# Block products of a row-tile pair formed with seven products instead of eight, in a fused autocorrelation and feed-forward kernel

## The chip, the cores and the metric

The kernel runs on one core of a Trainium2 chip, in float32 throughout. The metric is device time in microseconds, the median of several runs. Engines are named as the profile names them: PE (TensorE, the matmuls), DVE (VectorE), ACT (ScalarE), POOL (GpSimd) and SP (SyncE, which here only issues DMAs). They run beside each other, each in the order of its own instructions, and wait for each other on semaphores.

## The reference, cut to what matters

```python
def reference(x, w1q, a1, b1, w3q, a3, b3, w2q, a2, b2):      # x: (2, 2048, 1024)
    xn = _layernorm(x, axis=-1)
    # autocorrelation of each row, six best lags, weighted sum of the row shifted by them
    f = rfft(xn)
    corr = irfft(f * conj(f), n=1024)
    weights, delay = top_k(corr, 6)
    w = softmax(weights)
    s = sum_k(w[k] * xn[(t + delay[k]) % 1024])
    # gated feed-forward, weights repeated four times along the inputs, rank-2 additions
    q = lambda x, wq, A, B: x @ tile(wq, (1, 4)).T + 0.5 * (x @ A.T @ B.T)
    g = silu(q(silu(q(xn, w1q, a1, b1)) * q(xn, w3q, a3, b3), w2q, a2, b2))
    return x + s * g
```

The hidden width is 2752, a quarter of it 688, the row length 1024. There are 4096 rows.

## The kernel before

**Tiling.** Rows are taken 512 at a time, in 8 *macros* of 4 row tiles of 128. A macro's feed-forward works on columns: hidden values lie on partitions, the 512 rows along the free dimension. Because the weights repeat, the four quarters of the hidden vector are added up before the down product, so that it has an inner length of 688: five *chunks* of 128 (`zf[0]` to `zf[4]`) and a remainder of 48 with the two rank-2 rows, which is written twice, at partitions 0 and 64 (`zf[5]`).

**Steps.** A macro has 15 steps, written out in the last loop of the kernel. Steps 0 to 9 are `Ffn.up`: one chunk `c` in two steps, two quarters `j` in each step, four matmuls (0.86 us each) to a quarter. A quarter's two accumulators start from a *seed*, a scaled copy that ACT writes into the bank (L522); after the matmuls ACT takes Silu of the first (L549), DVE multiplies by the second (L551, "the z product"), and POOL adds the result into `zf[c]` (L554, L556). Step 10 is `up_rest`, the remainder in four accumulators (L573, L580, L590, L591). Steps 11 to 14 are `down(r)`, one row tile each: for both 512-column halves five matmuls of K=128 (L620) and one of K=64 (L631), then `out`: Silu on ACT (L642), times `s` on DVE (L643), plus `x` on POOL (L644), and the store. In the first of these steps `lora_mid` adds the rank-2 rows into `zf[5]` (L604, L607).

**Work between.** Each step has four lists of further work, `pre`, `mid`, `half` and `end`: ahead of the step's matmuls, after half of them, behind that, and behind the step. `plan` fills them by hand. They hold the next macro's norm (`stats`, `norm` with the folds `fold_a` and `fold_b`, `save` to DRAM twice over), its transposes (`turn`), the spectra (`power`: two matmul pairs, three ACT instructions, a DVE product and a POOL sum; every second one also joins two spectra, L386), and for each row tile `lags` (four matmuls, then the correlation row `corr`, L425 to L432, of which ACT writes the mirrored half) and `search` (MAX8 and FIND_INDEX8 on DVE). A row tile's six lags feed six gathers from DRAM (POOL's queue, L474, at most four in flight) and six weighted sums (`Gathers.sum`: the first on ACT, L488, five on DVE, L491); the list `sums` says how many are made at the half and at the end of each step. Macro 0 also makes its own spectra and searches (steps 0 to 5), and `lessen_part(c)` takes a row out of the first layer's weights, chunk by chunk (L137 on DVE, L138 on POOL).

**Buffers.** PSUM: two banks `ps` for transposes, spectra and lags, five `psf` (`full()`) for up and down accumulators, one `psu`. SBUF tiles with one tag share that tag's buffers. The order is the program's on each engine; DMAs of x, stores and weights are issued by SP, also in order, and a load waits there until its buffer is free.

Of the kernel before, what the change touches and what calls it, by code (L numbers as in the profile page):

```python
# [35 lines left out]
F32 = mybir.dt.float32  # L36
U32 = mybir.dt.uint32
I32 = mybir.dt.int32
AF = mybir.ActivationFunctionType
# [6 lines left out]
TOP = 6  # L46
# [22 lines left out]
def block_kernel(ctx: ExitStack, tc: tile.TileContext, x, w13t, w0t, w5t, w2t, a13, b13, b5, a2t, tf, ti, pick, out):  # L69
# [12 lines left out]
    p5 = pool("p5", ROLLS)  # L82
    small = pool("small", 3)
# [23 lines left out]
    w2_sb = const.tile([P, NC, L], F32)  # L107
    b5_sb = const.tile([P, 4], F32)
# [7 lines left out]
    b = const.tile([P, 513], F32, name="b")  # L116

    def constants():
        nc.gpsimd.memset(mhalf, -0.5)

        nc.scalar.activation(basef, mhalf, AF.Silu)
        nc.gpsimd.memset(euler, math.e)
        nc.gpsimd.memset(minus, -1.0)
        nc.gpsimd.memset(minus[0:1, :], 0.0)
        nc.gpsimd.memset(b[:, 512:513], 0.0)
        make_identity(nc, ident)
        nc.gpsimd.iota(base, pattern=[[0, 1]], base=0, channel_multiplier=2 * L)

    def fold_b(b, bcs):

        at = lambda first, par, n: bass.AP(b.tensor, b.offset + first, [list(b.ap[0]), [par, 2], [n, P]])
        nc.gpsimd.tensor_tensor(bcs[:, 0:2, :], at(0, 1, 2), at(512, -1, -2), ALU.subtract)
        nc.gpsimd.tensor_tensor(bcs[:, 2:4, :], at(2, -1, 2), at(510, 1, -2), ALU.add)
# [12 lines left out]
    def fold_lora(nat):  # L146

        pairs = p1.tile([P, 2, 8, 4], F32, tag="e2", name="a_pairs")
        nc.gpsimd.tensor_tensor(pairs, nat[:, 0], nat[:, 1], ALU.add)
        nc.gpsimd.memset(a13_sb, 0.0)  # L150
        whole = p1.tile([P, 8, 4], F32, tag="o2", name="a_whole")
        nc.gpsimd.tensor_tensor(whole[:, :2], pairs[:, 0, :2], pairs[:, 1, :2], ALU.add)
        nc.gpsimd.tensor_tensor(whole[:, 2:], pairs[:, 0, 2:], pairs[:, 1, 2:], ALU.subtract)
        nc.scalar.activation(a13_sb[:, :, :4], whole, AF.Copy, scale=0.125)


    class Corr:
# [25 lines left out]
        def norm(self, r, tags=("yc", "bcs")):  # L183
# [6 lines left out]
            yc = p1.tile([P, 4, P], F32, tag=tags[0], name=f"yc_{n}")  # L190
            bcs = p1.tile([P, 4, P], F32, tag=tags[1], name=f"bcs_{n}")
            nc.vector.tensor_tensor(a, xt[:, :512], xt[:, 512:], ALU.add)
            fold_a(a, yc, rest)
            nc.gpsimd.tensor_tensor(b[:, :512], xt[:, :512], xt[:, 512:], ALU.subtract)
# [43 lines left out]
        def lora_spread(self):  # L238
# [6 lines left out]
            self.u = p1.tile([P, NR], F32, tag="u", name=f"u_{self.m}")  # L245
# [79 lines left out]
        def lora_first(self, ffn):  # L325
# [3 lines left out]
            self.u = p1.tile([P, NR], F32, tag="u", name=f"u_{m}")  # L329
# [10 lines left out]
            for g, tags in enumerate((("ec", "e2"), ("zf2", "zf3"))):  # L340
                e = full(f"fe_{m}_{g}")
                self.wave(e, g, 0)
                ec, e2 = [p1.tile([P, NR], F32, tag=tag, name=f"{tag}_{m}_{g}") for tag in tags]
# [10 lines left out]
            nc.vector.tensor_copy(self.u, acc)  # L354
# [19 lines left out]
        def squares(self, g, ec, e2, o):  # L374
# [5 lines left out]
            o2 = p1.tile([P, NR], F32, tag="o2", name=f"o2_{m}_{g}")  # L380
# [3 lines left out]
            if g % 2:  # L384
                both = self.pwy if g == 1 else self.bT[:, 0:2, :]
                nc.gpsimd.tensor_tensor(both, both, to, ALU.add)  # L386

        def power(self, g):
# [4 lines left out]
            ec = p1.tile([P, NR], F32, tag="ec", name=f"ec_{m}_{g}")  # L393
            e2 = p1.tile([P, NR], F32, tag="e2", name=f"e2_{m}_{g}")
# [10 lines left out]
        def lags(self, r):  # L405
# [13 lines left out]
            corr = p1.tile([P, L], F32, tag="corr", name=f"corr_{n}")  # L419
# [43 lines left out]
    class Gathers:  # L463
# [15 lines left out]

        def sum(self, count):  # L480
            for _ in range(count):
                if not self.flying:
                    self.begin()
                st, r, k, g = self.flying.pop(0)
                w = st.w[:, r, k : k + 1]
                if k == 0:
                    s = self.s[st.m, r] = p3.tile([P, L], F32, tag="s", name=f"s_{st.m}_{r}")
# [6 lines left out]
    class Ffn:  # L494
# [69 lines left out]
        def up_rest(self, mid, half):  # L564
# [32 lines left out]
            nc.vector.tensor_tensor(last[:64, :], last[:64, :], zs[3][:64, :], ALU.add)  # L597

        def lora_mid(self):

            self.flush()
            last = self.zf[FULL]
# [6 lines left out]
        def down(self, r, mid, half):  # L609
            row = (self.m * RT + r) * P  # L610
            xs = []
            for d in range(2):
                xt = p2.tile([P, 512], F32, tag="x2", name=f"x2_{self.m}_{r}_{d}")
                nc.sync.dma_start(xt, x[row : row + P, d * 512 : (d + 1) * 512])
                xs.append(xt)
            accs = [full(f"y_{self.m}_{r}_{d}") for d in range(2)]
            rc = slice(r * P, (r + 1) * P)
            for d, acc in enumerate(accs):
                for c in range(FULL):
                    nc.tensor.matmul(  # L620
                        acc, lhsT=self.zf[c][:, rc], rhs=w2_sb[:, c, d * 512 : (d + 1) * 512], start=(c == 0), stop=False
                    )
                if d == 0:
                    if r == 0:
                        self.lora_mid()
                    mid()
                    half()

            for d, acc in enumerate(accs):
                at = slice(64 * d, 64 * d + 64)  # L630
                nc.tensor.matmul(  # L631
                    acc, lhsT=self.zf[FULL][at, rc], rhs=w2_sb[at, FULL, d * 512 : (d + 1) * 512], start=False, stop=True
                )
            return accs, xs

        def out(self, r, accs, xs, s):
            row = (self.m * RT + r) * P
            last = self.m == macros - 1 and r == RT - 1
            for d in range(2):
                cols = slice(d * 512, (d + 1) * 512)  # L640
                g = p2.tile([P, 512], F32, tag="g", name=f"g_{self.m}_{r}_{d}")
                nc.scalar.activation(g, accs[d], AF.Silu)  # L642
                nc.vector.tensor_tensor(g, s[:, cols], g, ALU.mult)  # L643
                (nc.vector if last else nc.gpsimd).tensor_tensor(g, g, xs[d], ALU.add)  # L644
                nc.sync.dma_start(out[row : row + P, cols], g)


    def plan(m, st, nxt, after, gathers, ffn_next):
# [3 lines left out]
        sums = [(1, 0)] * 7 + [(1, 2)] * 3 + [(1, 1), (0, 0), (2, 1), (2, 1), (0, 0)]  # L652
        sums[10] = (0, 0)
        sums[0], sums[1] = (0, 0), (1, 1)
        sums[8], sums[9], sums[11], sums[14] = (2, 1), (2, 1), (1, 0), (1, 0)
        if first:
            sums = [(0, 0)] * 7 + [(1, 1), (2, 1), (1, 1), (2, 2), (2, 2), (2, 1), (2, 1), (3, 0)]
            mid[0].append(st.odd_first)
            pre[1].append(lambda: st.power(2))
            mid[1].append(lambda: st.power(3))  # L660
            for r in range(RT):
                look(st, r, mid[2 + r], end[2 + r], gathers)
            mid[2 + RT].append(st.weights)
            for c in range(2, FULL + 1):
                pre[(0, 0, 1, 3)[c - 2]].append(lambda c=c: load_first(c))
                end[2 * c - 3].append(lambda c=c: lessen_part(c))
        else:
            end[0].append(st.weights)
        if nxt is not None:
            if first:  # L670
                loads, norms, turns = (None, None, None, 3), (0, 1, 4, 6), (mid[6], pre[7], mid[7], pre[8])
                stats = (half[0], half[1], end[2], half[5])

                tags = (("yc", "bcs"), ("zf4", "zf5"), ("e2", "o2"), ("yc", "bcs"))
            else:
                loads, norms, turns = (None, None, 1, 3), (0, 2, 4, 6), (pre[2], pre[4], pre[6], pre[8])
                stats = (half[0], end[1], end[3], end[5])
                tags = (("yc", "bcs"),) * RT
            for r in range(RT):
# [3 lines left out]
                end[norms[r]].append(lambda r=r: (nxt.norm(r, tags[r]), nxt.save(r)))  # L683
# [6 lines left out]
            pre[11].extend([nxt.again, nxt.lora_spread])  # L690
            for r in range(RT):
                look(nxt, r, mid[MID + 1 + r], end[MID + 1 + r], gathers)
# [243 lines left out]
```

## Time and profile before

| | |
|---|---|
| time, median of 3 runs | 1163.31 us (1163.22 to 1164.65) |
| the profiled execution's own time | 1167.36 us |
| its span, first to last instruction | 1165.6 us |
| granted PE clock, mean over the span | 0.994 of full speed |
| HBM read and written | 150.65 MB and 50.39 MB, 172 GB/s over the span |
| POOL's adds of L556 and L554 | 127.8 us and 51.8 us |
| POOL's folds L194, L132, L133 | 35.8, 25.5 and 28.8 us, 28 of each |
| POOL's joins L386 | 24.8 and 19.8 us, 8 of each |
| DVE's weighted sums L491 | 249.0 us, 160 of 1556 ns |

The page gives one profiled execution: busy time of each engine, the chain of work that ended last, the costliest groups of instructions by line and shape. A group's mean can hide two kinds of the same instruction, for instance alone and beside another engine, so single instructions are read from the timeline. PE is busy when a matmul is in flight; whether its clock was full is seen in the granted clock of a stretch. A float32 matmul of 128 x 512 shows as two records.

### The profile page before, as it was taken

To read this page: it belongs to the slowest core of one execution; us is meant where nothing else is said; L and a number is where in the kernel's file an instruction comes from. 1 tells how busy PE (TensorE), PEld (TensorE's weight loads), DVE (VectorE), ACT (ScalarE), POOL (GpSimd) and SP (SyncE) were. 2 spreads that over 40 slices of the span, in tenths; PEclk is the share of its full clock that TensorE was granted. 3 is DMA by queue.
4 is the path that set the end of the run, shared out by engine and by line. 5 is a ranking of instruction groups with operands and counts; after the bars stand their busy time and mean duration, and the time that the engine had idled before them with its cause. 6 is when DMAs were issued, how large, how long until landed. Compare 5 with 4: busy or idle time off the path is not lost.

```text
span 1165.6 us, 11210 instructions
## 1 busy us (share of the span) xinstructions
PE 1138.2 (98%) x3540; PEld 485.7 (42%) x3540; DVE 755.3 (65%) x1009; ACT 603.7 (52%) x1045; POOL 814.4 (70%) x675
## 2 busy tenths in 40 slices
PE   5999999999999999999999999999999999999997
PEld 4344344343444434444344433444344443444432
DVE  5587488665586746865577656785658765573455
ACT  4656623666346662566535664266633666344531
POOL 4778767877577884777767776787866877564653
PEclk9999999899999999999999999999999999999999
DMA  9941368534565435654355443754357534452334
GB/s 364 372 151 75 109 203 293 184 132 145 163 214 183 142 130 180 217 181 162 128 175 201 169 160 109 236 207 147 118 157 237 181 127 155 144 190 90 119 116 162
DMA packets 64915, 201.78 MB, mean 173 GB/s; under 512 B 7612, under 2 KB 7868, under 8 KB 64088
## 3 DMA queue, kind: packets, MB, share of 16 engines
q0 software_dynamic: 27648, 100.68, 26.9%
q1 hardware_dynamic: 37208, 100.39, 23.9%
q8 instruction: 28, 0.46, 0.2%
q14 instruction: 31, 0.25, 0.1%
HBM read 150.65 MB, written 50.39 MB: 172 GB/s over the span
## 4 chain that ended last, share of the span: by engine, by line
PE 87%; DVE 7%; POOL 2%; ACT 2%; issue 2%; DMA 0%; DVEq 0%; ACTq 0%; POOLq 0%
PE gu L544 44%; PE y L620 21%; PE u L527 4%; PE y L631 3%; PE gu L580 2%; PE t L216 2%; PE gu L573 2%; DVE s L491 1%; PE fe L369 1%; PE fe L372 1%; PE fo L369 1%; PE o L414 1%; PE fo L372 1%; PE ua L232 1%; PE e L414 1%
## 5 line engine op out<-in xcount | busy, mean ns | idle before, releaser
L544 PE MATMUL gu<-yT,w_sb 128*128 128x512 f32 x960 | 460.5, 601 | 0.1
L620 PE MATMUL y<-w_sb,zf 128*128 128x512 f32 x640 | 287.5, 597 | 0.5 <-ACT g L642 0.5
L544 PEld LDWEIGHTS gu<-yT,w_sb 128*128 128x128 f32 x960 | 176.8, 191 | 233.9 <-issue 214.4
L474 POOL DMA_INDIRECT roll<-scr,lag x192 | 230.2, 1199 | 47.4 <-issue 33.3
L491 DVE SCALAR_TENSOR_TENSOR s<-roll,w,s 128x1024 f32<-128x1024 f32 x160 | 249.0, 1556 | 7.2 <-DMA roll<-scr,lag 4.3
L551 DVE TENSOR_TENSOR z<-z,gu 128x512 f32<-128x512 f32 x160 | 109.2, 683 | 175.9 <-PE gu L544 118.0
L522 ACT ACTIVATE gu<-second,b_sb 128x512 f32<-128x512 f32 x320 | 207.6, 684 | 10.2 <-DVE z L551 9.3
L549 ACT ACTIVATE z<-gu 128x512 f32<-128x512 f32 x160 | 95.3, 596 | 177.8 <-PE gu L544 176.2
L620 PEld LDWEIGHTS y<-w_sb,zf 128*128 128x128 f32 x640 | 117.3, 190 | 147.8 <-issue 144.7
L644 POOL TENSOR_TENSOR g<-g,x 128x512 f32<-128x512 f32 x62 | 101.8, 1661 | 94.2 <-DVE g L643 88.5
L544 PE MATMUL gu<-yU,w_sb 128*128 128x512 f32 x320 | 163.8, 593 | 0.0
L556 POOL TENSOR_TENSOR zf<-zf,z 128x512 f32<-128x512 f32 x80 | 127.8, 1598 | 21.5 <-DVE z L551 20.3
L554 POOL TENSOR_TENSOR zf<-z,z 128x512 f32<-128x512 f32 x40 | 51.8, 1295 | 85.9 <-DVE z L551 84.2
L544 PEld LDWEIGHTS gu<-yU,w_sb 128*128 128x128 f32 x320 | 61.1, 191 | 77.2 <-issue 73.6
L643 DVE TENSOR_TENSOR g<-s,g 128x512 f32<-128x512 f32 x64 | 41.6, 690 | 67.5 <-ACT g L642 67.4
L450 POOL TENSOR_TENSOR e<-euler,e 128x6 f32<-128x6 f32 x32 | 45.8, 1431 | 41.8 <-DVE e L449 40.0
L642 ACT ACTIVATE g<-y 128x512 f32<-128x512 f32 x64 | 34.8, 593 | 77.3 <-PE y L631 59.6
L432 ACT COPY corr<-corr 128x511 f32<-128x511 f32 x32 | 19.8, 619 | 79.7 <-DVE corr L431 79.7
L527 PE MATMUL u<-z,a_sb 128*2 128x512 f32 (+1 forms) x384 | 52.9, 591 | 2.0 <-DVE z L551 2.0
L143 DVE SCALAR_TENSOR_TENSOR yc<-a,rest 128x256 f32<-128x256 f32 x28 | 41.6, 1487 | 5.3 <-POOL rest L188 2.0
L515 ACT ACTIVATE gu<-second,b_sb 64x512 f32<-64x512 f32 x64 | 43.9, 686 | 1.7
L418 ACT COPY oc<-o 128x258 f32<-128x258 f32 x32 | 12.0, 375 | 63.0 <-PE o L414 62.8
(167 smaller groups left out, 1358.9 us busy)
## 6 DMA issues: line engine op xcount, KB each, us to landing
scr<-x SPq DMA_DIRECT2D x64, 512.0 KB
x<-in_x SPq DMA_DIRECT2D x32, 512.0 KB
x<-in_x SPq DMA_DIRECT2D x64, 256.0 KB
out<-g SPq DMA_DIRECT2D x64, 256.0 KB
w_sb<-in_w13t SPq DMA_DIRECT2D x5, 1024.0 KB
second<-rows SPq DMA_DIRECT2D x14, 256.0 KB
w_sb<-in_w2t SPq DMA_DIRECT2D x1, 3072.0 KB
roll<-scr,lag POOLq DMA_INDIRECT x192, 5.7
```

What stands on the lines that cost most here:

```text
L450: nc.gpsimd.tensor_tensor(e, bass.AP(euler.tensor, euler.offset, [list(euler.ap[0]), [0, TOP]]), e, ALU.pow)
L474: nc.gpsimd.indirect_dma_start(out=g, out_offset=None, in_=st.scratch[r].rearrange("p (n o) -> (p n) o", o=1), in_offset=bass.IndirectOffs ...
L491: nc.vector.scalar_tensor_tensor(s, g, w, s, ALU.mult, ALU.add)
L522: nc.scalar.activation(acc, self.st.second[:, wi, :], AF.Copy, scale=b13_sb[:, c, q : q + 1])
L527: nc.tensor.matmul(self.u2[32 * j : 32 * j + 2, :], lhsT=a2_sb[:rows, 4 * c + j, :], rhs=z[:rows, :], start=(c == 0), stop=(c == FULL),)
L544: nc.tensor.matmul(acc, lhsT=w13_sb[:, c, 2 * j + wi, k, :], rhs=y, start=False, stop=(k == 1), skip_group_check=True,)
L549: nc.scalar.activation(z, accs[0], AF.Silu)
L551: nc.vector.tensor_tensor(z, z, accs[1], ALU.mult)
L554: nc.gpsimd.tensor_tensor(self.sum_of(c), zs[0], zs[1], ALU.add)
L556: nc.gpsimd.tensor_tensor(self.zf[c], self.zf[c], z, ALU.add)
L620: nc.tensor.matmul(acc, lhsT=self.zf[c][:, rc], rhs=w2_sb[:, c, d * 512 : (d + 1) * 512], start=(c == 0), stop=False)
L644: (nc.vector if last else nc.gpsimd).tensor_tensor(g, g, xs[d], ALU.add)
```

## The change

1. `down` and `out` of one row tile become `down_head`, `down_tail` and `out` of a *pair* of row tiles, q = 0 in steps 11 and 12, q = 1 in steps 13 and 14. Chunks 0 to 3 are treated as two 2 x 2 block products (chunks 0 and 1, chunks 2 and 3; blocks are two row tiles by two chunks and two chunks by two column halves), in the form of Winograd: seven products instead of eight, added in four banks. The copy of P1 to a second bank and of P7 to SBUF is ACT's, two sums into banks are DVE's. Chunk 4 and the remainder stay as they are; the two remainder matmuls of a pair now take two row tiles instead of two halves.
2. The combinations of the left side (`mix`: four DVE instructions of 128 x 256 for each pair of chunks) are made at the ends of steps 8 and 9; those of the weights once, on POOL (`mix_weights`: four instructions of 128 x 1024), in macro 0's steps 6 and 7.
3. `b` and `fold_b` move from POOL to DVE; `join` is split from `squares` and moves from POOL to DVE, to step 10 (step 1 in macro 0).
4. `again` and `lora_spread` move from ahead of step 11 to its end; `lora_mid`, with the last sum of `up_rest` in it, to the end of step 11.
5. `search` moves ahead of the outputs of a step, `sums` and macro 0's norms, stats and `lessen_part` are spread anew.
6. x tiles for the output have a pool of three, shared with the spectra; the output is written over x. `corr`, `o2`, `ec`, `e2`, the fourth `s` and others take other buffers.

```diff
     def fold_b(b, bcs):
...
-        nc.gpsimd.tensor_tensor(bcs[:, 0:2, :], at(0, 1, 2), at(512, -1, -2), ALU.subtract)
-        nc.gpsimd.tensor_tensor(bcs[:, 2:4, :], at(2, -1, 2), at(510, 1, -2), ALU.add)
+        nc.vector.tensor_tensor(bcs[:, 0:2, :], at(0, 1, 2), at(512, -1, -2), ALU.subtract)
+        nc.vector.tensor_tensor(bcs[:, 2:4, :], at(2, -1, 2), at(510, 1, -2), ALU.add)
...
+    B = lambda k, n: w2_sb[:, :4, :].rearrange("p (a k) l -> p a k l", k=2)[:, :, k, n * 512 : (n + 1) * 512]
+    T1, T2, T3, T4 = B(0, 1), t_sb[:, 0], t_sb[:, 1], t_sb[:, 2]
+    mix_weights = [
+        lambda: nc.gpsimd.tensor_tensor(T3, B(1, 1), B(0, 1), ALU.subtract),
+        lambda: nc.gpsimd.tensor_tensor(T1, B(0, 1), B(0, 0), ALU.subtract),
+        lambda: nc.gpsimd.tensor_tensor(T2, B(1, 1), T1, ALU.subtract),
+        lambda: nc.gpsimd.tensor_tensor(T4, B(1, 0), T2, ALU.subtract),
+    ]
...
             nc.vector.tensor_tensor(a, xt[:, :512], xt[:, 512:], ALU.add)
+            nc.vector.tensor_tensor(b[:, :512], xt[:, :512], xt[:, 512:], ALU.subtract)
             fold_a(a, yc, rest)
-            nc.gpsimd.tensor_tensor(b[:, :512], xt[:, :512], xt[:, 512:], ALU.subtract)
...
-            if g % 2:
-                both = self.pwy if g == 1 else self.bT[:, 0:2, :]
-                nc.gpsimd.tensor_tensor(both, both, to, ALU.add)
+        def join(self, g):
+            both, to = ((self.pwy, self.cT), (self.bT[:, 0:2, :], self.bT[:, 2:4, :]))[g // 2]
+            nc.vector.tensor_tensor(both, both, to, ALU.add)
...
+        def mix(self, a):
...
+            nc.vector.tensor_tensor(S1, A(1, 0), A(1, 1), ALU.add)
+            nc.vector.tensor_tensor(S2, S1, A(0, 0), ALU.subtract)
+            nc.vector.tensor_tensor(A(1, 0), A(0, 0), A(1, 0), ALU.subtract)
+            nc.vector.tensor_tensor(S4, A(0, 1), S2, ALU.subtract)
...
+        def down_head(self, q, mid, half):
+            self.q, self.xs = q, {}
+            for i, n in ((0, 0), (1, 0), (0, 1)):
+                self.load_x(i, n)
...
+            self.ys = [full(f"y_{self.m}_{2 * q + i}_{n}") for n in range(2) for i in range(2)]
+            y00, y10, y01, y11 = self.ys
+            self.add_to(y01, p1_, True)
+            nc.scalar.copy(y00, y01)
+            self.add_to(y11, p7_, True)
+            self.p7 = p5.tile([P, NR], F32, tag="z", name=f"p7_{self.m}_{q}")
+            nc.scalar.copy(self.p7, y11)
+            self.add_to(y01, p6_)
+            nc.vector.tensor_tensor(y10, y01, self.p7, ALU.add)
+            self.flush()
+            mid()
+            half()
+            self.add_to(y00, p2_)
+            self.add_to(y00, self.plain(0, 0))
+
+        def down_tail(self, mid, half, s, between):
...
+            self.add_to(y01, p5_)
+            nc.vector.tensor_tensor(y11, y01, self.p7, ALU.add)
+            mid()
+            half()
+            self.add_to(y10, p4_)
+            self.add_to(y10, self.plain(1, 0))
+            self.rest(0, (y00, y10))
+            self.out(0, 0, y00, s)
+            self.load_x(1, 1)
+            self.out(1, 0, y10, s)
+            between()
+            self.add_to(y01, p3_)
+            self.add_to(y01, self.plain(0, 1))
+            self.add_to(y11, self.plain(1, 1))
+            self.rest(1, (y01, y11))
+            self.out(0, 1, y01, s)
+            self.out(1, 1, y11, s)
...
+            nc.scalar.activation(g, acc, AF.Silu)
+            nc.vector.tensor_tensor(g, s(i)[:, cols], g, ALU.mult)
+            (nc.vector if last else nc.gpsimd).tensor_tensor(xt, g, xt, ALU.add)
+            nc.sync.dma_start(out[row : row + P, cols], xt)
...
+        sums = [(0, 0), (1, 1), (1, 0)] + [(1, 1)] * 4 + [(2, 1)] * 3 + [(1, 1), (1, 0), (0, 0), (1, 0), (0, 0)]
         if first:
-            sums = [(0, 0)] * 7 + [(1, 1), (2, 1), (1, 1), (2, 2), (2, 2), (2, 1), (2, 1), (3, 0)]
+            sums = [(0, 0)] * 6 + [(0, 1), (1, 1), (2, 2), (2, 2), (2, 2), (1, 0), (1, 0), (2, 2), (3, 0)]
+            for at, f in zip((half[6], end[6], half[7], end[7]), mix_weights):
+                at.append(f)
...
+            half[1].append(lambda: st.join(0))
+            end[1].append(lambda: st.join(2))
...
-                end[2 * c - 3].append(lambda c=c: lessen_part(c))
+                half[2 * c - 1].append(lambda c=c: lessen_part(c))
...
-                loads, norms, turns = (None, None, None, 3), (0, 1, 4, 6), (mid[6], pre[7], mid[7], pre[8])
+                loads, norms, turns = (None, None, None, 3), (half[1], end[1], end[4], end[6]), (mid[6], pre[7], mid[7], pre[8])
...
-            pre[11].extend([nxt.again, nxt.lora_spread])
+            half[10].append(lambda: nxt.join(0))
+            end[10].append(lambda: nxt.join(2))
+            end[MID + 1].extend([nxt.again, nxt.lora_spread])
             for r in range(RT):
-                look(nxt, r, mid[MID + 1 + r], end[MID + 1 + r], gathers)
-            mid[STEPS - 1].insert(0, lambda: (ffn_next.seed(0), ffn_next.seed(1, (0,))))
+                look(nxt, r, mid[MID + 1 + r], (mid[MID + 2], between[MID + 2], end[MID + 3], half[MID + 4])[r], gathers)
+            mid[STEPS - 1].insert(0, lambda: ffn_next.seed(0, (0,)))
+            between[MID + 4].append(lambda: (ffn_next.seed(0, (1,)), ffn_next.seed(1, (0,))))
             end[STEPS - 1].insert(0, lambda: ffn_next.seed(1, (1,)))
+        for a in range(2):
+            end[8 + a].append(lambda a=a: ffns[m].mix(a))
+        end[MID + 1].append(ffns[m].lora_mid)
```

Here `y` indices are row tile of the pair, then column half; `add_to` issues two matmuls for a product (one for each pair of chunks), `plain` one for chunk 4, `rest` the two K=64 matmuls.

## The prediction

> **What bounds the kernel now.** I read the page's busy shares first, then the chain that ended last, then the timelines of PE and DVE at one place in several macros, and last the windows with the granted clock.
>
> ```profile
> PE 1138.2 (98%) x3540; PEld 485.7 (42%) x3540; DVE 755.3 (65%) x1009; ACT 603.7 (52%) x1045; POOL 814.4 (70%) x675
> PE 87%; DVE 7%; POOL 2%; ACT 2%; issue 2%; DMA 0%; DVEq 0%; ACTq 0%; POOLq 0%
> ```
>
> PE is the bound. The 13% of the chain that is not PE lies almost all before 215 us. From macro 1 on the same event comes back at an exact distance, which the chain in order of time shows (start, length):
>
> ```profile
> 294.42 4.29 PE y L620 x10
> ...
> 434.03 4.29 PE y L620 x10
> ...
> 573.64 4.29 PE y L620 x10
> ```
>
> The period is 139.61 us, PE without a gap. So from macro 1 to 7 each PE microsecond removed is a microsecond of time, if no new wait eats it. An f32 matmul leaves two records; ten records in 4.29 us make 0.858 us a matmul.
>
> **What is removed.** A pair of row tiles needs 2 tiles x 2 column halves x 4 chunks = 16 block matmuls; after, 7 products x 2 = 14. The fifth chunk and the K=64 remainder stay (4 and 2x2 for a pair). Two pairs a macro: 4 x 0.858 = 3.43 us a macro, **27.5 us in 8**. Every other term is what is given back.
>
> **Where each bank stands.** down_head holds four of the five psf banks, so which it gets first matters. In macro 0 the first y group starts at 144.86 while the four z products of L591 run until 149.43: it takes the one bank that up_rest leaves free. A second row says how banks are dealt out:
>
> ```profile
> 186.90 4.56 PE L620 MATMUL y<-w_sb,zf 128*128 128x512 f32 x10 [0.53 <-ACT g L642]
> ```
>
> This is y_3_1, waiting for the Silus of tile 2. By order of full() calls its bank would be that of y_1_0, free since 172; by order of first writes (y_3_0, three seeds, y_3_1) it is y_2_1's, which fits. So after the change P1 in y01, the first write, takes the free bank and doesn't wait; the copy into y00 gets the bank of up_rest's z 0, P7 (y11) that of z 1, the sum into y10 that of z 2.
>
> **The turn of step 10 to 11, macros 1 to 6** (times of macro 3, ahead of the change):
>
> ```profile
> 569.95 0.69 DVE L382 TENSOR_TENSOR bT<-ec,fo 128x512 f32<-128x512 f32 x1 [3.89 <-ACT o L381]
> 570.67 1.30 DVE L591 TENSOR_TENSOR z<-z,gu 64x512 f32<-64x512 f32 x2
> ...
> 572.52 1.12 PE L244 MATMUL u<-us,pick_sb 128*128 128x512 f32 x2
> 573.48 4.46 PE L620 MATMUL y<-w_sb,zf 128*128 128x512 f32 x10
> ```
>
> Between L382 and the z products DVE now has a sum and join(0). No DVE join is in the trace: its nearest rows are a 1024-wide sum, 1.28 alone, 1.79 where POOL adds beside it (129.97), and twice a 512-wide sum, 1.2. z 1 ends at 570.6 + 1.3 to 1.8 + 1.2 + 1.3 = 574.4 to 575.0. lora_spread has moved behind, so P1 starts at 572.45, P7 wants its bank at 574.17: a **new wait of 0.3 to 0.9, I take 0.5**. Behind it P7 to 576.5, P6 to 578.2 (the copy into y00, 0.59 on ACT, lies beside P7), a2 to 579.2; lags(0) needs join(2), which stands behind z 2, z 3 and another sum: 579.1 to 579.6. **I take 0.3.** Together 0.8.
>
> The rest of the down steps, followed in the same way, is hidden: y10 and y11 sums (0.69 as L643) are wanted 5 and 4 us later; lora_mid (0.7 + 4 x 0.69 on DVE, then the ACT copy) ends some 2 us before the remainder; search (2.85) ahead of the outputs makes mirror copy L432, then Silu, late by about 1.5, but y banks are asked for only in the next head. The tightest is the copy into the next y00: it stands on ACT behind the Silu of (1,1), whose g buffer waits for POOL's add (1.66) of (1,0). It ends about 0.5 before P6 wants it. At the macro's end the last seed comes some 2 us before its matmul.
>
> **Folds, mixes, loads.** The norm of a tile costs DVE today 0.69 + 1.51 + 1.07 = 3.27 beside POOL's L194, L132, L133. Alone, the two yc lines take:
>
> ```profile
> 9.76 0.48 DVE L143 SCALAR_TENSOR_TENSOR yc_yc<-a,rest 128x256 f32<-128x256 f32 x1
> 10.16 0.42 DVE L144 TENSOR_TENSOR yc_yc<-a 128x256 f32<-128x256 f32 x1
> ...
> 627.85 1.51 DVE L143 SCALAR_TENSOR_TENSOR yc<-a,rest 128x256 f32<-128x256 f32 x1
> 629.29 1.07 DVE L144 TENSOR_TENSOR yc<-a 128x256 f32<-128x256 f32 x1
> ```
>
> With POOL idle, a, b, yc x2, bcs x2 are 2 x 0.69 + 0.48 + 3 x 0.42 = 3.12 (fold_b by the reversed L428, 0.42): nothing is added. Were all as slow as beside POOL it would be 1.5 + 2.6 + 2.1 = 6; I take the first, since what slowed them leaves POOL with them. The Trainium skill speaks against moving more two-input work to DVE: GPSIMD Engine Reference, 1. Specifications, has DVE instructions with two SBUF inputs contend with GpSimd. The new ones are all such, but POOL also loses 3.2 a norm and the 3.1 joins, which today stretch two sums to 5.08. DVE gains a macro 8 x 0.42 (mix) + 2.5 (joins) + 2.8 (y sums) and loses some 5 of contention: 94 of 139 become 98 to 103, with z products late by at most 4, where about 5.5 are borne (the seed of quarter j+3 wants z j's bank: two quarters of 3.43 less two seeds of 0.69). Two sums in steps 3 to 6 put 7 us of DVE beside 7.9 of PE. Mix lies in DVE's gap of 2.6 before 549.93. ACT gets two copies a head, 4 x 0.59 = 2.4 a macro in an engine that is half idle. I cost all this at nothing: what hides it is PE's own 0.86 a matmul; if that cover fails, a z product is late, the seed behind it too, and PE loses about 1 in such a step. SP gets load_x(1,1), waiting until the output of (0,0) has landed, with the next outputs behind it: POOL's last add comes late, with nothing for PE behind it but norms with slack. lora_spread's three small DMAs come 13 us later and have 25 us left. Only **in macro 7** that load sits on the end: output landed at 6.5 after the remainder, x landed at 9, add and store: 1.5 more (0 to 2).
>
> **Macro 0** is bound by DVE and POOL, and gets the most edits. lessen_part moves half a step to one step nearer to its use, behind the mix weights on POOL. Followed on from the trace: step 4's weights cost PE 0.4, step 6's 2.2. In step 7 POOL has z's add (1.3), a gather (1), T2 (2.4, as L138), then the lessening of chunk 4 (2.4), done near 111; PE wants it at 105: **5 us**. Before, PE loses about 6.6 in the same stretch (1.2 at 47, 0.8 at 73, 4.6 around 94). In step 10 chunk 5 stands behind two sums and two gathers: 3.2; P7 behind two sums, 2.6; lags(0) 1.2; P3 1.9 behind search 2; the second seed of macro 1, behind Silus that wait for POOL, 4. Before, 8.0 are lost there (1.9, 0.5, 2.8, rest half clock).
>
> For half clock the windows view gives the row (stretch, length, then busy per engine, then PEclk):
>
> ```profile
> 154.02:157.43 3.41, 1.86 (x5) 0.55 (x3) 3.27 (x5) 0.00 (x0) 2.25 (x3) 1.00 1.02 305
> 157.43:160.84 3.41, 3.09 (x7) 1.27 (x8) 2.27 (x5) 2.21 (x4) 0.00 (x0) 1.00 0.82 297
> 205.24:208.65 3.41, 1.21 (x3) 0.19 (x1) 2.01 (x3) 3.41 (x6) 3.15 (x3) 1.00 0.39 162
> 208.65:212.06 3.41, 2.81 (x9) 1.96 (x10) 3.41 (x5) 2.66 (x6) 3.23 (x4) 0.50 0.88 298
> ```
>
> After 1.86 busy the clock stays, after 1.21 it halves for such a stretch, 1.7 us lost. The Trainium skill, TensorE: Matmul & The Clock Gate, Part 1, asks for a whole idle window of about 3.4: by it none of these stalls but step 8's would cost clock; by the row a stall from 2 does in about half of the cases. I take the row: 3 to 4 such windows in macro 0, about as before plus 2. By the rule macro 0 would gain 3. Sum for macro 0: the 3.43 are eaten and **2 more** (from -4 to +8).
>
> **Sum**, from the profiled execution's 1167.4 (span 1165.6 and 1.8 around it): macros 1 to 6, 6 x (3.43 - 0.8) = -15.8; macro 7, -3.43 + 1.5 = -1.9; macro 0, +2. Together -15.7: 1151.7 profiled. The median of the runs shown is 4.05 lower, 1163.31: **1148**, on its own 1142 to 1155.
>
> **Rivals.**
> *Slower: the first product waits.* If banks went by order of calls, P1 would stand in z 1's bank: 2.2 a macro instead of 0.5, and in a 3.41 window that leaves 1.2 busy, so mostly half clock, 1.7. From 3.43 for the two together a macro is slower than today. 3.9 + 0.3 in six macros is +4.6, macro 0 +4, macro 7 -1.9: about 1170. For it: PE is in order, and the trace has no stall whose size tells this. Against: the 186.90 row. 16%.
> *Heads that wait each for ACT.* The 0.5 of slack at the second head is thin, POOL's add goes up to 2.3 beside DVE. 0.7 lost in each of 14 heads: +10 on the forecast, 1158. 17%.
> *All is hidden.* The 0.8 vanish and macro 0 keeps its 3.43, because its stalls only take the place of old ones: 1163.3 - 27.5 + 1.5 = 1137. 14%.
> *It removes less:* if the form needed further matmuls to add its products, PE records would not fall; accumulation in banks and two DVE sums replace them, so 2%, at 1163.
> The forecast has 51%.
>
> A measurement here tells 0.2% (2.3 us) from no change. Faster takes the forecast, the hidden case, most of the heads case: 0.76; same 0.07; slower 0.17. The range takes in the hidden case below and the heads case and its edge above: 1137 to 1164.
>
> **What would show it.** L620's successor with 8 x 36 x 2 = 576 records at 0.43; a period of 136.5 to 137.5 from macro 1 to 6; DVE z 1 ahead of P7's bank with a wait below 1; yc rows at 0.5; in macro 0 a PE gap before chunk 4's products that ends with POOL's lessening. A period of 139 or more, or clock digits below 9 in each macro, would make it wrong.

## The result and the profile after

The changed kernel takes 1169.96 us in the median (13 runs) beside 1164.76 us of the kernel before: a ratio of 1.0043, 95% interval 1.0030 to 1.0057. It is slower by 5 us; 1148 was forecast. Its runs go from 1164.53 to 1172.35 us, and the two below 1165 us have a granted clock of 0.988 where the others have 0.982 to 0.985. Its profiled execution has a span of 1168.4 us and a mean granted clock of 0.984. The profiled executions took 1170.27 and 1167.36 us, so between the two traces only 2.9 us are to be found; that of the kernel before lay 2.6 us above its median.

The busy shares and the chain by engine, from the page of the changed kernel:

```profile
PE 1117.5 (96%) x3476; PEld 473.2 (40%) x3476; DVE 820.6 (70%) x1204; ACT 620.8 (53%) x1077; POOL 719.9 (62%) x607
PE 79%; DVE 9%; issue 4%; POOL 4%; ACT 2%; DMA 1%; POOLq 0%; DVEq 0%; SPq 0%; ACTq 0%
```

The 64 records that were to go have gone (3540 to 3476), and PE is busy for 20.7 us less. Yet the span is 2.8 us longer, and the chain holds 79% of PE where it held 87%: what was removed, and more, came back as time in which PE stands. The chain in order of time (start, length) says where it did not:

```profile
355.66 13.93 PE gu L567 x32
492.73 13.93 PE gu L567 x32
629.80 13.93 PE gu L567 x32
766.87 13.93 PE gu L567 x32
```

The period is 137.07 us, 2.54 below the 139.61 of before. The first of these rows (macro 2) has its counterpart in the chain of the kernel before:

```profile
338.32 13.93 PE gu L544 x32
```

So the changed kernel reaches macro 2 **17.3 us late** and then wins 14.5 until the end. PE's timeline gives the times at which it reaches the same work in macro 0 (the last column is the first experiment's):

| PE reaches (us) | before | after | difference | early lessening |
|---|---|---|---|---|
| rank-2 products of chunk 0, step 2 | 56.18 | 54.60 | -1.6 | 54.45 |
| rank-2 products of chunk 1, step 4 | 73.20 | 82.20 | +9.0 | 72.34 |
| rank-2 products of chunk 2, step 6 | 90.74 | 105.79 | +15.1 | 89.03 |
| rank-2 products of chunk 3, step 8 | 114.81 | 133.50 | +18.7 | 112.08 |
| first products of step 10 | 133.75 | 153.93 | +20.2 | 134.32 |
| macro 1 | 192.45 | 210.69 | +18.2 | 192.27 |
| macro 2 | 338.32 | 355.66 | +17.3 | 337.50 |
| end of the span | 1165.6 | 1168.4 | +2.8 | 1150.4 |

All of it is lost from step 4 to step 10 of macro 0. PE's timeline of the changed kernel there (start, length; in brackets the idle time before it and what ended that):

```profile
76.79 2.07 PE L567 MATMUL gu<-yT,w_sb 128*128 128x512 f32 x2 [7.27 <-POOL w_sb L143]
...
98.21 1.10 PE L567 MATMUL gu<-yT,w_sb 128*128 128x512 f32 x2 [2.65 <-ACT gu L545]
100.37 2.08 PE L567 MATMUL gu<-yT,w_sb 128*128 128x512 f32 x2 [1.06 <-POOL w_sb L143]
...
122.58 1.12 PE L567 MATMUL gu<-yT,w_sb 128*128 128x512 f32 x2 [1.61 <-DVE w_sb L142]
128.08 2.08 PE L567 MATMUL gu<-yT,w_sb 128*128 128x512 f32 x2 [4.37 <-POOL w_sb L143]
```

L142 and L143 are the lessening, its DVE and its POOL half: chunks 2, 3 and 4 each start with PE waiting for their own weights. Only the row at 98.21 names something else, a seed on ACT. By the kernel's order, though, the seeds that ACT writes then (from 97.39) are those of the quarter after, and chunk 3's half of the lessening on DVE ends at 98.11, just ahead of the matmul:

```profile
96.26 1.85 DVE L142 SCALAR_TENSOR_TENSOR w_sb<-w,minus,w_sb 128x1024 f32<-128x1024 f32 x1
```

In the rows at 76.79, 100.37 and 128.08 two matmul records take 2.07 or 2.08 us where 1.02 is usual; the windows from there on (stretch, length, then busy of PE, PEld, DVE, ACT, POOL, then the granted clock) show why:

```profile
76.79:82.20 5.41, 5.41 (x6) 1.84 (x6) 0.00 (x0) 1.79 (x3) 2.49 (x2) 0.50 0.47 167
100.37:105.79 5.42, 5.42 (x6) 1.85 (x7) 1.30 (x3) 1.79 (x3) 4.84 (x3) 0.50 0.00 0
128.08:133.50 5.42, 5.42 (x7) 1.85 (x8) 4.55 (x1) 1.79 (x3) 5.22 (x3) 0.50 0.00 0
```

Each of the three is the start of 5.4 us at half clock, 2.7 us lost. And why the first stall is 7.3 us long stands in POOL's timeline:

```profile
65.89 1.35 POOL L468 TENSOR_TENSOR e<-euler,e 128x6 f32<-128x6 f32 x1 [1.27 <-DVE e L467]
67.43 1.99 POOL L492 DMA_INDIRECT roll<-scr,lag  x1 [0.20 <-issue]
69.72 0.94 POOL L492 DMA_INDIRECT roll<-scr,lag  x1 [0.30 <-issue]
70.97 0.93 POOL L492 DMA_INDIRECT roll<-scr,lag  x1 [0.30 <-issue]
72.21 0.94 POOL L492 DMA_INDIRECT roll<-scr,lag  x1 [0.30 <-issue]
73.17 1.27 POOL L579 TENSOR_TENSOR zf<-zf,z 128x512 f32<-128x512 f32 x1
74.39 2.34 POOL L143 TENSOR_TENSOR w_sb<-w_sb,w 128x1024 f32<-128x1024 f32 x1
```

The lessening of chunk 2 has moved from the end of step 1 to the half of step 3. The four gathers of row tile 0, issued at the start of step 3, are now ahead of it, and they wait for search 0 (L468). In the kernel before the same instruction stands ahead of the gathers, the first of which starts at 71.88:

```profile
57.52 2.35 POOL L138 TENSOR_TENSOR w_sb<-w_sb,w 128x1024 f32<-128x1024 f32 x1
```

In macros 1 to 6 the turn of step 10 to 11 looks as it was foretold; PE and DVE of macro 3:

```profile
587.31 1.98 PE L651 MATMUL y<-w_sb,zf 128*128 128x512 f32 x4
589.59 1.96 PE L651 MATMUL y<-t_sb,zf 128*128 128x512 f32 x4 [0.29 <-DVE z L614]
...
594.52 0.71 PE L432 MATMUL o<-ti_sb,bT 128*128 128x129 f32 x4 [0.29 <-DVE bT L404]
```

The same turn on DVE:

```profile
586.90 1.21 DVE L404 TENSOR_TENSOR pwy<-pwy,cT 128x1024 f32<-128x1024 f32 x1
588.15 2.51 DVE L614 TENSOR_TENSOR z<-z,gu 64x512 f32<-64x512 f32 x4
590.57 1.69 DVE L514 SCALAR_TENSOR_TENSOR s<-roll,w,s 128x1024 f32<-128x1024 f32 x1
592.19 2.28 DVE L404 TENSOR_TENSOR bT<-bT 128x1024 f32<-128x1024 f32 x1
```

P1 (587.31) doesn't wait, P7 waits 0.29 for z 1, lags(0) 0.29 for the second join.

### The profile page after: what moved, and what is told of

It is laid out like the page before. It is cut to its first block, busy times and chain, and to the rows that moved or that the text cites. A ratio compares the mean times of both kernels' runs of the same rounds, so it can differ in the third digit from the quotient of the medians.

```text
span 1168.4 us, 11257 instructions
## 1 busy us (share of the span) xinstructions
PE 1117.5 (96%) x3476; PEld 473.2 (40%) x3476; DVE 820.6 (70%) x1204; ACT 620.8 (53%) x1077; POOL 719.9 (62%) x607
## 4 chain that ended last, share of the span: by engine, by line
PE 79%; DVE 9%; issue 4%; POOL 4%; ACT 2%; DMA 1%; POOLq 0%; DVEq 0%; SPq 0%; ACTq 0%
PE gu L567 45%; PE y L651 16%; PE u L550 3%; PE y L661 2%; DVE s L514 2%; PE t L234 2%; PE fe L385 1%; PE o L432 1%; DVE bT L404 1%; PE fo L385 1%; PE fe L388 1%; PE e L432 1%; DMA x<-in_x 1%; PE ua L250 1%; PE gu L603 1%
## 5 line engine op out<-in xcount | busy, mean ns | idle before, releaser
L567 PE MATMUL gu<-yT,w_sb 128*128 128x512 f32 x960 | 465.5, 606 | 17.5 <-POOL w_sb L143 12.7
L492 POOL DMA_INDIRECT roll<-scr,lag x192 | 236.9, 1234 | 45.6 <-issue 31.9
L514 DVE SCALAR_TENSOR_TENSOR s<-roll,w,s 128x1024 f32<-128x1024 f32 x160 | 238.3, 1490 | 4.0 <-DMA roll<-scr,lag 3.1
L579 POOL TENSOR_TENSOR zf<-zf,z 128x512 f32<-128x512 f32 x80 | 132.6, 1657 | 70.4 <-DVE z L574 69.6
L651 PE MATMUL y<-w_sb,zf 128*128 128x512 f32 x256 | 123.5, 605 | 0.0
L733 POOL TENSOR_TENSOR x<-g,x 128x512 f32<-128x512 f32 x62 | 84.2, 1368 | 59.8 <-DVE g L732 37.8
L468 POOL TENSOR_TENSOR e<-euler,e 128x6 f32<-128x6 f32 x32 | 48.5, 1516 | 113.2 <-DVE e L467 101.6
L577 POOL TENSOR_TENSOR zf<-z,z 128x512 f32<-128x512 f32 x40 | 65.5, 1638 | 61.2 <-DVE z L574 56.6
L651 PEld LDWEIGHTS y<-w_sb,zf 128*128 128x128 f32 x256 | 46.9, 193 | 60.7 <-issue 60.7
L651 PE MATMUL y<-t_sb,zf 128*128 128x512 f32 x128 | 60.7, 596 | 2.0 <-DVE z L614 2.0
L651 PE MATMUL y<-w_sb,S 128*128 128x512 f32 x128 | 61.8, 605 | 0.0
```

The costliest lines, as they stand in the source:

```text
L468: nc.gpsimd.tensor_tensor(e, bass.AP(euler.tensor, euler.offset, [list(euler.ap[0]), [0, TOP]]), e, ALU.pow)
L492: nc.gpsimd.indirect_dma_start(out=g, out_offset=None, in_=st.scratch[r].rearrange("p (n o) -> (p n) o", o=1), in_offset=bass.IndirectOffs ...
L514: nc.vector.scalar_tensor_tensor(s, g, w, s, ALU.mult, ALU.add)
L567: nc.tensor.matmul(acc, lhsT=w13_sb[:, c, 2 * j + wi, k, :], rhs=y, start=False, stop=(k == 1), skip_group_check=True,)
L577: nc.gpsimd.tensor_tensor(self.sum_of(c), zs[0], zs[1], ALU.add)
L579: nc.gpsimd.tensor_tensor(self.zf[c], self.zf[c], z, ALU.add)
```

## The experiments

Ratios are to the kernel before, measured with each run (medians 1164.65 to 1165.73 us); "below the changed kernel" is the difference to its median of 1169.96 us.

**Early lessening.** Only the place of the lessenings is undone in the changed kernel.

```diff
-                half[2 * c - 1].append(lambda c=c: lessen_part(c))
+                end[2 * c - 3].append(lambda c=c: lessen_part(c))
```

> The changed kernel with the four lessenings of macro 0 back at the ends of steps 1, 3, 5 and 7, all else as changed. Theory (the loss is POOL's queue in macro 0: the first layer's weights of chunks 2, 3 and 4 are lessened behind four gathers, a norm and T2, and the stalls of 7.3, 2.7 + 1.1 and 1.6 + 4.4 us leave about 2.7 us of half clock each): these three stalls and their half clock go, about 24 us in all, of which some 5 to 8 come back as the small waits that the kernel before has there; 1150 to 1154 us, and step 10 of macro 0 is reached near 136 us instead of 153.9. Rival (macro 0 is bound by the sum of DVE's and POOL's work, to which folds, joins and mixed weights have been added, and a stall taken away comes back in the next step): step 10 still after 146 us, time 1162 or more.

Measured: **1151.76 us**, 0.9890 of before (0.9875 to 0.9905), so 18.2 below the changed kernel; step 10 at 134.32. The three stalls for weights are gone; PE's timeline has these in their place between 40 us and step 11:

```profile
65.27 1.98 PE L567 MATMUL gu<-yT,w_sb 128*128 128x512 f32 x4 [0.93 <-ACT gu L545]
90.57 1.02 PE L550 MATMUL u<-z,a_sb 128*2 128x512 f32 x2 [0.51 <-DVE z L574]
103.26 0.66 PE L234 MATMUL t<-ident,yc 128*128 128x128 f32 x4 [2.90 <-ACT cT L238]
126.85 0.64 PE L385 MATMUL fe<-yT,tf_sb 128*64 128x512 f32 x1 [2.88 <-ACT e L414]
143.13 2.08 PE L388 MATMUL fo<-bT,tf_sb 128*128 128x512 f32 x2 [3.03 <-DVE bT L398]
```

They sum to 10.3 us, where before has 1.23 and 1.95 and half clock. The theory holds: macro 0 is not bound by its sum of work, the place of four instruction pairs cost 18 us.

**Chunk 2 alone.**

```diff
-                half[2 * c - 1].append(lambda c=c: lessen_part(c))
+                (end[1] if c == 2 else half[2 * c - 1]).append(lambda c=c: lessen_part(c))
```

> The changed kernel with only chunk 2's lessening back at the end of step 1. Theory (each stall stands for itself): the 7.3 us before chunk 2's products and the 2.9 us of half clock behind it go, about 1 comes back at the end of step 1: 1160 to 1162 us, while the stalls before chunks 3 and 4 stay at about 3.7 and 6 us. Rival (a macro 0 bound by DVE and POOL gives it back): the stalls before chunks 3 and 4 grow by about as much, time 1166 or more.

Measured: 1160.51 us (0.9964, 0.9952 to 0.9976), 9.5 below the changed kernel. The later stalls stay: 2.65 and 1.07 before chunk 3, 1.59 and 4.36 before chunk 4. Each stall stands for itself.

**The gathers alone.** The lessening stays where the change has put it; the gathers ahead of it go.

```diff
-                gathers.begin()
+                if (m, p) != (0, 3):
+                    gathers.begin()
```

> The changed kernel, in which step 3 of macro 0 issues no gathers; the four of row tile 0 are issued at step 4, behind the lessening of chunk 2, which stays where the change has put it. Theory (of the 7.3 us stall before chunk 2's products the four gathers, 67.4 to 73.2 on POOL, make 5 to 6): the stall falls to 1 to 2.5 us, most of the 2.7 us of half clock behind it goes; macro 2 starts 6 to 9 us earlier, 1161 to 1164 us. Rival (the lessening waits for search 0's power, not for the gathers, or the later gathers hold up the sums): the stall stays above 4, 1167 or more.

Measured: 1164.21 us (0.9989, 0.9981 to 0.9996), 5.8 below the changed kernel and just above the range expected; in its profiled execution macro 2 starts at 346.83, 8.8 earlier. The start of chunk 2 on PE:

```profile
71.79 1.12 PE L567 MATMUL gu<-yT,w_sb 128*128 128x512 f32 x2 [2.30 <-POOL w_sb L143]
```

And its lessening on POOL, at 74.39 in the changed kernel:

```profile
69.39 2.35 POOL L143 TENSOR_TENSOR w_sb<-w_sb,w 128x1024 f32<-128x1024 f32 x1
```

The stall falls from 7.27 to 2.30, and with it the half clock: the matmuls take 1.12. So 5.0 us of it were the gathers. Half clock comes back at chunk 3, where PE's timeline has

```profile
90.56 4.24 PE L567 MATMUL gu<-yT,w_sb 128*128 128x512 f32 x4 [2.67 <-ACT gu L545]
```

In the changed kernel the stall of 2.65 us at this place was followed by two records at full clock (1.10); here one of 2.67 us is followed by 0.50 at once. The profiled execution took 1161.36 us, 2.9 below the median of its 22 runs, which go from 1159.78 to 1166.37 us while the granted clock goes from 0.989 to 0.985. So the 8.8 us of the trace and the 5.8 us of the medians differ by how much half clock a run meets; where in the slower runs is not shown, since they have no trace.

**The mixed weights later.**

```diff
-            for at, f in zip((half[6], end[6], half[7], end[7]), mix_weights):
+            for at, f in zip((half[8], end[8], half[9], end[9]), mix_weights):
```

> The changed kernel with the four combinations of the weights on POOL moved from steps 6 and 7 to steps 8 and 9 of macro 0. Theory (at chunk 4 T2, 2.35 us, stands ahead of the lessening): the 4.4 us stall falls to about 2, and with it perhaps 1 of half clock; chunk 5's lessening then has up to 4.7 us more ahead of it in step 9, which shows as a wait at step 10 of up to 4 instead of 1.3: 1165 to 1170 us, nearly no gain. Rival (the mixed weights are the larger part of macro 0's loss): below 1162.

Measured: 1168.38 us (1.0036, 1.0023 to 1.0049), no difference from the changed kernel that the intervals tell, as the theory has it. What it won before chunk 4 was given back two steps later:

```profile
124.02 1.12 PE L567 MATMUL gu<-yT,w_sb 128*128 128x512 f32 x2 [2.08 <-POOL w_sb L143]
...
151.94 3.78 PE L596 MATMUL gu<-yT,w_sb 128*128 128x512 f32 x4 [4.03 <-POOL w_sb L143]
```

Chunk 4 now waits 2.1 us at full clock, but step 10 waits 4.0 instead of 1.3, with half clock (3.78 for four records).

**Gathers ahead of the search at the turn to macro 1.** There PE stands 5.6 us for a seed (221.69) in the changed kernel.

```diff
                 gathers.sum(sums[p][1])
+                if m == 0 and p > MID:
+                    gathers.begin()
                 for f in end[p]:
```

> The changed kernel with the gathers of macro 0's steps 11 to 14 issued ahead of the step's search, not behind it. Theory (at the turn to macro 1 the last gathers stand on POOL behind the power of search 2, which waits for DVE; so the last sums, search 3, the products with s, POOL's adds and ACT's Silus all come late, and the seeds behind them cost PE 5.6 us and about 3 of half clock): the gathers come 4 to 5 us earlier, the stall falls to 1 to 2, the half clock goes: 1162 to 1165 us. Rival (the end of macro 0 is bound by the number of DVE's instructions there, three sums, a search and four products in step 14): the stall stays above 4, 1168 or more.

Measured: 1166.78 us (1.0009, 0.9996 to 1.0023), 3.2 below the changed kernel; the stall is 2.91 and half clock remains. Both expectations missed: the late gathers make half of the stall. By DVE's timeline the rest stands behind the search (209.20 to 212.16), whose products with `s` follow it only then.

**The lessening alone, in the kernel before.** The same edit the other way round.

```diff
-                end[2 * c - 3].append(lambda c=c: lessen_part(c))
+                half[2 * c - 1].append(lambda c=c: lessen_part(c))
```

> The kernel before with one edit of the change alone: the lessenings of chunks 2 to 5 at the halves of steps 3, 5, 7 and 9 instead of the ends of steps 1, 3, 5 and 7. Theory (it is this edit that cost macro 0 its time): PE stalls before the products of chunks 2, 3 and 4, the first behind gathers on POOL, of 10 to 15 us with half clock; 1174 to 1181 us. Rival (the later lessening only hurts together with the mixed weights and the other moved work): 1164 to 1169 us.

Measured: **1183.31 us**, 1.0149 of before (1.0133 to 1.0164), 18.4 us more, above the upper end that was expected. PE's timeline:

```profile
79.61 2.08 PE L544 MATMUL gu<-yT,w_sb 128*128 128x512 f32 x2 [7.27 <-POOL w_sb L138]
101.49 4.24 PE L544 MATMUL gu<-yT,w_sb 128*128 128x512 f32 x4 [3.59 <-ACT gu L522]
```

The stall before chunk 2 has the same 7.27 us without products of seven, mixed weights or folds on DVE. Undone in the one kernel and done in the other, the edit is worth 18 us; this settles the cause.

**Folds back on POOL**, on top of the early lessenings: `b` and `fold_b` as before the change.

```diff
-            nc.vector.tensor_tensor(b[:, :512], xt[:, :512], xt[:, 512:], ALU.subtract)
             fold_a(a, yc, rest)
+            nc.gpsimd.tensor_tensor(b[:, :512], xt[:, :512], xt[:, 512:], ALU.subtract)
...
-        nc.vector.tensor_tensor(bcs[:, 0:2, :], at(0, 1, 2), at(512, -1, -2), ALU.subtract)
-        nc.vector.tensor_tensor(bcs[:, 2:4, :], at(2, -1, 2), at(510, 1, -2), ALU.add)
+        nc.gpsimd.tensor_tensor(bcs[:, 0:2, :], at(0, 1, 2), at(512, -1, -2), ALU.subtract)
+        nc.gpsimd.tensor_tensor(bcs[:, 2:4, :], at(2, -1, 2), at(510, 1, -2), ALU.add)
```

> The changed kernel with the early lessenings (1151.8 us) and, besides, b and fold_b back on POOL. Theory (folds on DVE neither give nor cost PE anything in macros 1 to 7): period 137.0 to 137.2, 1149 to 1154 us; the yc rows go back to 1.0 to 1.5 us where POOL folds beside them. Rival (without the folds on DVE, its work beside POOL is too slow and z products come late): period above 137.5, 1156 or more.

Measured: 1159.27 us (0.9940, 0.9927 to 0.9954), 7.5 more than without this edit. Macro 2 starts 6.2 us later (343.68), and the period is 137.7 us in three of five macros: to the two waits of 0.29 comes, in macro 3, one of 0.42 for a spectrum's product (L398). The rival's numbers hold, its reason in part: most of the loss is ahead of macro 2, where the stalls of the early lessening have grown (1.54 instead of 0.51 for a z product, 4.41 instead of 2.88 at a spectrum's matmuls), and in the later macros it is a spectrum's product that is late, not a z product. The `yc` rows of L148, 0.47 us each with the folds on DVE, take 1.55 with them on POOL. That folds moved to DVE is not neutral, as I had it: it gives.

**Three edits at once**: early lessenings, gathers ahead of the search, and in macros 1 to 7

```diff
-        sums = [(0, 0), (1, 1), (1, 0)] + [(1, 1)] * 4 + [(2, 1)] * 3 + [(1, 1), (1, 0), (0, 0), (1, 0), (0, 0)]
+        sums = [(0, 0), (1, 1), (1, 0)] + [(1, 1)] * 4 + [(2, 1)] * 3 + [(0, 0), (1, 1), (1, 0), (1, 0), (0, 0)]
```

> Three edits on the changed kernel at once: the lessenings back at the ends of steps 1, 3, 5 and 7; the gathers of macro 0's steps 11 to 14 ahead of the search; and in macros 1 to 7 the two weighted sums of step 10 moved to the end of step 11 and the half of step 12. Theory (the pieces add up: 18.2 and 3.2 us as measured alone, and the two waits of 0.29 a macro at steps 10 to 11, which stand behind those two sums on DVE, go: 6 to 7 times 0.58 = 3.5 to 4): 1144 to 1147 us, period 136.5 instead of 137.07. Rival (the sums only push the outputs of step 12, so that a bank comes free later): period 137.0 or more, 1148 or more.

Measured: 1155.88 us (0.9915, 0.9901 to 0.9928), a miss: worse than the early lessenings alone. The two waits of 0.29 are gone, but PE's timeline of macro 3 shows a new one at the second head:

```profile
595.79 1.98 PE L651 MATMUL y<-t_sb,S 128*128 128x512 f32 x4 [1.49 <-ACT y L691]
```

And ACT ahead of it:

```profile
593.44 0.60 ACT L731 ACTIVATE g<-y 128x512 f32<-128x512 f32 x1 [4.29 <-POOL x L733]
594.66 0.60 ACT L731 ACTIVATE g<-y 128x512 f32<-128x512 f32 x1 [0.62 <-POOL x L733]
595.15 0.59 ACT L691 COPY y<-y 128x512 f32<-128x512 f32 x1
```

P6 waits for the copy of P1, which stands on ACT behind Silus that wait for POOL's adds. Period 137.94 = 137.07 - 0.58 + 1.49, within 0.04. This is the rival of the heads that wait for ACT. What has delayed the adds is not the moved sum's 1.3 us on DVE: the products with `s` start 1.8 us behind POOL's L468 in both kernels (588.70 after 586.88 here, 606.76 after 604.93 in the changed kernel). It is POOL's queue. Behind a sum at the half of a step the kernel also issues the gathers that are ready (`gathers.begin()` in `others`), so the moved sum brought three gathers into step 12. They take POOL from 588.44 to 592.11, and the first add follows at 592.14, 3.4 us after its product began. In the changed kernel no gather stands there, and the add starts 0.8 us after its product began (607.53). It is the trap of chunk 2 once more.

**Mixed weights spread**, on top of the last:

```diff
-            for at, f in zip((half[6], end[6], half[7], end[7]), mix_weights):
+            for at, f in zip((half[5], end[6], half[7], end[8]), mix_weights):
```

> As the kernel with the three edits, and the mixed weights on POOL at the half of step 5, the end of 6, the half of 7 and the end of 8 instead of the halves and ends of 6 and 7. Theory (in macro 0 a run of POOL adds, T2, z, T4 and the lessening of chunk 5, holds a sum of DVE up, and T3 holds up the norm whose transposes PE waits 2.9 us for): 2 to 5 us less than the kernel with the three edits, 1140 to 1144; no sum on DVE in steps 7 and 8 above 4 us. Rival (macro 0 has no room on POOL at all, the waits only change place): within 1.5 us of that kernel.

Measured: 1153.07 us (0.9889, 0.9874 to 0.9904), 2.8 below the last; the absolute time missed because of the 1.49 above. Macro 2 starts at 333.10 instead of 336.32, and the longest sum on DVE in this stretch is 3.74 us, as expected.

**Five edits.** Early lessenings, spread weights, gathers ahead of the search, macro 0's last search behind the outputs, and a sum of step 10 moved to where DVE has room:

```diff
-        sums = [(0, 0), (1, 1), (1, 0)] + [(1, 1)] * 4 + [(2, 1)] * 3 + [(1, 1), (1, 0), (0, 0), (1, 0), (0, 0)]
+        sums = [(0, 0), (1, 1), (1, 1)] + [(1, 1)] * 4 + [(2, 1)] * 3 + [(0, 1), (1, 0), (0, 0), (1, 0), (0, 0)]
...
-                look(nxt, r, mid[MID + 1 + r], (mid[MID + 2], between[MID + 2], end[MID + 3], half[MID + 4])[r], gathers)
+                look(nxt, r, mid[MID + 1 + r], (mid[MID + 2], between[MID + 2], end[MID + 3], (end if first else half)[MID + 4])[r], gathers)
```

> Five edits on the changed kernel: early lessenings; mixed weights spread over steps 5 to 8; macro 0's gathers ahead of the search in steps 11 to 14; its last search behind the outputs of step 14; and in macros 1 to 7 one of step 10's two sums moved to the end of step 2. Theory (step 2 has 7.9 us of PE and only one sum beside the norm, so the sum is free there, and both waits of 0.29 go without a new one at the second head; at the turn to macro 1 the Silus no longer wait for search 3): period 136.5, the 3.7 us wait at the turn below 1.5 with no half clock: 1138 to 1142 us. Rival (the copy into y00 waits at the second head as it did with the sums moved to step 12): period 137.3 or more, 1145 or more.

Measured: **1140.99 us**, 0.9787 of before (0.9769 to 0.9805); it beats both kernels. Its chain:

```profile
468.28 13.93 PE gu L567 x32
604.64 13.93 PE gu L567 x32
741.00 13.93 PE gu L567 x32
```

The period is 136.36, and PE has no wait left in macro 3. Of the 3.43 us that were removed a macro, 3.25 arrive. At the turn to macro 1 the expectation missed: the wait for a seed (3.73 us in the last run) is gone, but one of 2.28 us for a norm's `yc` has come, with half clock behind it, and macro 2 starts at 331.92, only 1.2 us earlier than in the last run.

## Why the prediction was wrong

**What held.** The seven products: 64 records fewer, 3.43 us a macro. The banks go by first writes: P1 never waits in macros 1 to 6, P7 does for z 1. The two waits, 0.5 and 0.3 in the prediction, are 0.29 each, and the period is 137.07, inside the 136.5 to 137.5 named. (139.61 - 3.43 + 0.58 is 136.76; where the other 0.3 goes is not shown.) From macro 2 to the end -14.5 us was measured; -12.7 for five macros and -1.8 for the last, where -13.2 and -1.9 were forecast. The slack of the second head was thin, as said, and three edits at once broke it.

**The step that failed is macro 0, "2 more (from -4 to +8)".** Measured: 17.3 late at macro 2; if macro 1 wins the 2.54 of the later ones, macro 0 has lost 19.9. Together with some 0.7 by which macros 1 to 7 fell short, that is the whole miss between the two traces, +2.9 us instead of -15.7. It failed in three places.

1. "Step 4's weights cost PE 0.4." They cost 7.27, plus 2.7 of half clock. The prediction has the lessening moved by half a step to one step; by the diff it is one and a half. And of the moved lessening I counted its own time and the mixed weights ahead of it, not the four gathers that the start of step 3 puts on the same queue, nor the search that they wait for. 5.0 us of the stall are theirs, by the run without them. At chunk 4, where the queue was listed instruction by instruction, a gather included, 5 us were forecast and 6.0 measured.
2. The half clock. I took 3 to 4 windows of 1.7 us, "about as before plus 2". Adding busy time times what the clock lacks, over 40 to 240 us, gives 12.3 us after and 4.7 before. The Trainium skill (TensorE: Matmul & The Clock Gate, Part 1) wants a whole idle window; the stall at 98 to 100 us, 2.65 and 1.06 with 1.1 of work between, has none of 3.4 and is followed by 5.42 us at 0.50, and so is the 2.67 alone in the run with the gathers later. The row was right against the rule, and I still booked too little by it.
3. The sum. The stalls that I listed for macro 0 add up to 20.5, with half clock some 26.5; less the 3.43 removed and the 14.6 that before loses, that is about +8.5. I wrote +2, as if each stall swallowed part of the next. The experiments with chunk 2 alone and with the gathers alone show that they don't: taking one away leaves the others their size.

The other terms of that list were too small or too large by less: step 6 2.2, measured 3.7; step 8 5, measured 6.0; step 10 3.2, measured 1.3 and 1.0; P7 2.6, measured 0.24; lags(0) 1.2, measured 1.4; P3 1.9, measured none; the seed of macro 1 4, measured 5.6.

With the lessenings back in place macro 0 costs 337.50 - 338.32 + 2.5 = 1.7 us, and the time is 0.989 of before: 1150.5 on the scale of the forecast's 1148. So one edit, priced at 0.4, 2.2 and 5 us ahead of chunks 2, 3 and 4, makes the difference of 18 us. That the rest comes so near to +2 is in part luck: the waits of that kernel, 10.3 us up to step 11, are not the ones in my list.

**Folds and joins "at nothing"** held for PE in macros 1 to 6 of the changed kernel but for the two waits: the six records of a, b and the folds sum to 3.1 us (macro 1, 228.09 to 230.78), yc rows are back at 0.48 and 0.42. But the run with folds on POOL is 7.5 us slower, so nothing was too low a value for what they give. **The rivals**: none was right. The slower one named about 1170 us, which is the time measured, but by luck: it put its loss into each macro, into a first product that waits, and P1 waits nowhere. The loss lies in macro 0 alone.

## What to carry to other kernels

An instruction that is moved later in program order joins its engine's queue behind everything issued in between, DMA issues included; list that queue instruction by instruction, with what its first one waits for, before pricing the move. Price the first pass of a pipelined kernel by itself, add its stalls up, and add half clock behind the longer ones. Their length alone doesn't tell which: 2.30 us cost none here and 2.67 us in the same run did, while 2.90 us with the early lessening did not. The gain of seven passes was lost in the first. When a sum is moved off a tight spot, look for the step whose PE time exceeds DVE's work, not for the next one in line, and see what else the program issues with it.

## What the hardware showed unexpectedly

A weighted sum on DVE with two SBUF inputs takes 1.28 us alone. In the changed kernel one was hit by a run of POOL adds; DVE's timeline:

```profile
123.05 9.57 DVE L514 SCALAR_TENSOR_TENSOR s<-roll,w,s 128x1024 f32<-128x1024 f32 x1
```

And POOL's:

```profile
123.39 2.35 POOL L168 TENSOR_TENSOR t_sb<-w_sb 128x1024 f32<-128x1024 f32 x1
125.69 2.34 POOL L143 TENSOR_TENSOR w_sb<-w_sb,w 128x1024 f32<-128x1024 f32 x1
127.98 1.26 POOL L579 TENSOR_TENSOR zf<-zf,z 128x512 f32<-128x512 f32 x1
129.20 2.34 POOL L169 TENSOR_TENSOR t_sb<-w_sb,t_sb 128x1024 f32<-128x1024 f32 x1
```

POOL's four instructions end at 131.54, the sum at 132.62. 1.28 and the run's 8.15 make 9.43: it is as if the sum stood still for the whole run, where I had reckoned with rows half as long again. The run with the mixed weights later tests this. The same sum, behind the same z product, has there only two POOL adds beside it, from 121.60 to 125.17, and takes 4.99 us (from 121.28). POOL's run is 4.58 us shorter (3.57 for 8.15), and so is the sum (4.99 for 9.57). What in the two engines makes DVE wait is not shown here.
